# Expert weights applied on the way out of PSUM, results added to x by accumulating gathers, block scales on GpSimd, and weight rounding placed between the experts' tiles

## The chip, the cores and the metric

One core of a Trainium2 chip runs the whole kernel. The metric is the device time of one launch in microseconds (us); lower is better. The engines are TensorE (PE; its weight loads are PEld), VectorE (DVE), ScalarE (ACT), GpSimd (POOL) and SyncE (SP, which issues DMAs).

## What is computed

Four decoder layers on x of 8 sequences x 256 tokens x 256 features, all in 32 bit. Each layer adds self-attention, cross-attention and a feed-forward block to x. The change touches two neighbours: the feed-forward block of layer 1 (32 experts, the best 4 for each token, and a shared expert) and the attention of layer 2, whose operands are rounded to eight-bit floats in blocks of 128.

```python
def _L1_ffn_ref(x, ...):
    scores = softmax(flat @ router_w.T + router_bias)
    topk_scores, topk_idx = top_k(scores, 4)
    topk_scores = topk_scores / clip(topk_scores.sum(-1), 1e-12)
    h = silu(einsum('nd,ehd->neh', flat, gate_w)) * einsum('nd,ehd->neh', flat, up_w)
    expert_out = einsum('neh,edh->ned', h, down_w)
    sel = take_along_axis(expert_out, topk_idx[:, :, None], axis=1)
    out = (sel * topk_scores[:, :, None]).sum(axis=1)
    return out + silu(flat @ sgate_w.T) * (flat @ sup_w.T) @ sdown_w.T

def quant_dequant(x, maxval, fp8_dtype):          # blocks of 128, row-major
    s = max(abs(flat), axis=1) / maxval
    return (flat / s).astype(fp8_dtype).astype(float32) * s

def _L2_attn_ref(x, Wq, Wk, Wv, Wo, ln_w, ln_b):
    xn = fp8_layernorm(x, ln_w, ln_b)             # rounds its input (e4m3)
    q, k, v = (fp8_linear(xn, W) for W in (Wq, Wk, Wv))   # rounds xn and W (e4m3)
    qd, kd = qd_e5m2(rope(q)), qd_e5m2(rope(k))
    probs = softmax(qd @ kd.T / sqrt(D))
    return fp8_linear(probs @ v, Wo)
...
x = x + _L1_ffn_ref(layernorm(x), ...)
x = x + _L2_attn_ref(layernorm(x), ...)
```

## The kernel before

x stays in SBUF as eight tiles, one for each sequence, each of two halves of 128 tokens. The normalised x (xn) and its transpose (xnT) are also resident. Weights come through a ring of three slots.

The feed-forward block of layer 1 first writes xn to a table xd in HBM (one row for each token) and loads all experts' weights into one tile `wall`. `route` picks four experts for each token, gives each (token, expert) pair a place in a list sorted by expert, padded to tiles of 128 places, and makes three things: `place` (for each token, its four places), `token` (for each place, its token; 0 in places that nobody uses) and `who` (for each of the 96 tiles, the offset of its expert's weights). It also collects the four routing weights of each token in `w4`. Beside it the shared expert's sixteen steps run on TensorE, fourteen of them interleaved with the route by hand and two after the tiles.

`tiles_of_experts` then goes over the 96 tiles in a pipeline of four parts, each one step later than the one ahead of it: `turn` gathers 128 rows of xd (an indirect DMA that GpSimd issues) into xg and transposes them on TensorE, `widen` multiplies with gate and up weights whose offset TensorE reads from a register, `flip` transposes h, `narrow` multiplies with the down weights, copies the product out of PSUM on ACT as y, and SP writes y to a second table yd. In this stage only TensorE's order is fixed to program order; the other engines' instructions are ordered by the scheduler.

The attention of layer 2 is a list of generators, one for each sequence and one for rounding the weights. `staggered` runs them in turns: turn n takes one step of each work that has started, the oldest first; sequence b starts at turn 10 b, the weights at turn 0. Each `yield` ends a step. Here all four engines keep exactly the program's order (`in_order`; the profile shows these instructions under L71). A sequence's steps are: `expert_results` (eight gathers from yd into six buffers g, and eight VectorE steps that multiply with w4 and add to x), two rounds of moments, inverse root of the variance (GpSimd) and `e4m3` rounding, projections, rotation of q and k with the `scales` of e5m2 rounding, scores, softmax, values, `e4m3` again, output projection, and the statistics for the next layer. `scales` takes a block's largest magnitude, divides it by the format's largest number and inverts it, all on VectorE; `e4m3` is `scales`, four ACT steps (y = x times the inverse scale), four VectorE steps (rounding) and four ACT steps (times the scale), with a `yield` after each.

## Time and profile before

| | |
|---|---|
| three timed runs | 2462.15, 2464.55, 2473.96 us; median 2464.55 us |
| the profiled execution | 2461.47 us, span from first to last instruction 2459.7 us |
| busy in the span | PE 2217.8 (90%), DVE 1245.0 (51%), ACT 872.7 (35%), POOL 501.0 (20%) us |
| tiles of experts | first gather 1267.8 us, last write of y issued 1436.0 us |
| rounded attention | first gather from yd 1438.6 us, last statistics on GpSimd 1716.9 us |
| HBM traffic | 84.64 MB read, 16.78 MB written |

How to read the rows. A group has the line of the kernel, the engine and operation, the tiles written and read, shape and count; after the bar the busy time in us and the mean ns of one; after the second bar how long the engine had been idle just before, and what ended that. A wait row says which instruction waited for which: us in total, times, longest. A timeline row begins with the start and the length in us, and has the idle time before it in brackets. Busy shares are means over stages that have different owners, so each stage is looked at by itself.

### The profile page before, as it was taken

Reading aid. Unit: us, or ns where it says so; the run is one execution under the profiler, and the core shown is the slowest. Engines: PE = TensorE matmul, PEld = TensorE weight load, DVE = VectorE, ACT = ScalarE, POOL = GpSimd, SP = SyncE. Lnnn points to the kernel's source line nnn. Section 1 sums busy time; section 2 is a strip of 40 time slices with the busy share of each in tenths; the row PEclk is TensorE's granted clock in tenths of the full one; section 3 lists DMA queues with packets and bytes.
Section 4 is the critical chain, followed back from the end, with each engine's and each line's share of the span. In section 5 each row is a group of like instructions: output and inputs, shape, how many; then the busy total and the mean of one; then the engine's idle time right before and its main releaser. Section 6 shows DMA issues by size and latency. Waiting matters only on the chain. (4 is left out here: it accounts for less than half of the span.)

```text
span 2459.7 us, 31787 instructions
## 1 busy us (share of the span) xinstructions
PE 2217.8 (90%) x11611; PEld 1410.8 (57%) x11611; DVE 1245.0 (51%) x3192; ACT 872.7 (35%) x2118; POOL 501.0 (20%) x712
## 2 busy tenths in 40 slices
PE   7888889999999999899899955666999989999999
PEld 4555555666655555555568833444665555566556
DVE  5666553334323235676565558985453235555500
ACT  3433422334211113466113335664552114434311
POOL 3211333221000002221135534440222110000010
PEclk9999999999999999899899976886899998899999
DMA  3000000001100000121515643100111010000000
GB/s 128 1 1 1 30 14 26 18 10 41 52 13 26 13 18 13 48 66 36 210 53 165 153 95 104 46 18 14 49 39 32 1 52 10 18 18 18 3 13 22
DMA packets 56539, 103.68 MB, mean 42 GB/s; under 512 B 7624, under 2 KB 40224, under 8 KB 54720
## 3 DMA queue, kind: packets, MB, share of 16 engines
q1 hardware_dynamic: 44688, 75.90, 9.0%
q0 software_dynamic: 7680, 20.98, 3.7%
q10 hardware_dynamic: 4016, 4.76, 0.6%
q8 instruction: 94, 1.54, 0.3%
q14 instruction: 61, 0.50, 0.1%
HBM read 84.64 MB, written 16.78 MB: 41 GB/s over the span
## 5 line engine op out<-in xcount | busy, mean ns | idle before, releaser
L169 PE MATMUL mm<-xnT,w 128*128 128x512 f32 (+1 forms) x1104 | 475.3, 577 | 1.4 <-ACT xnT L252 0.7
L345 PE MATMUL mm<-kT,qT 17*128 17x256 f32 (+2 forms) x1536 | 322.4, 413 | 15.7 <-DVE q L363 12.7
L169 PEld LDWEIGHTS mm<-xnT,w 128*128 128x128 f32 x1104 | 210.6, 193 | 201.2 <-issue 192.1
L376 PE MATMUL mm<-qT,kT 18*128 18x256 f32 (+2 forms) x1536 | 309.5, 406 | 1.4 <-ACT p L388 1.2
L388 ACT ACTIVATE p<-mm 128x512 f32<-128x512 f32 (+1 forms) x384 | 212.1, 562 | 262.0 <-PE mm L376 137.1
L363 DVE TENSOR_REDUCE q<-mm 128x2 f32<-128x512 f32 x256 | 172.3, 688 | 164.1 <-PE mm L376 148.7
L345 PEld LDWEIGHTS mm<-kT,qT 17*128 17x128 f32 (+1 forms) x1536 | 179.1, 193 | 115.0 <-issue 41.3
L560 ACT ACTIVATE hT<-mm 128x512 f32<-128x512 f32 x104 | 62.1, 597 | 431.0 <-PE mm L169 416.6
L561 DVE TENSOR_TENSOR hT<-hT,mm 128x512 f32<-128x512 f32 x104 | 71.4, 687 | 278.2 <-PE mm L169 278.1
L536 PE MATMUL acc<-w,hT 128*128 128x256 f32 x832 | 195.5, 379 | 1.0 <-DVE x L271 1.0
L536 PEld LDWEIGHTS acc<-w,hT 128*128 128x128 f32 x832 | 157.9, 190 | 62.9 <-issue 41.6
L376 PEld LDWEIGHTS mm<-qT,kT 18*128 18x128 f32 (+1 forms) x1536 | 172.3, 191 | 13.2 <-issue 4.6
L235 POOL TENSOR_SCALAR rstd<-mv 128x2 f32<-128x2 f32 x64 | 12.3, 193 | 812.7 <-DVE mv L231 466.8
L399 PE MATMUL acc<-p,v 128*32 128x256 f32 (+2 forms) x1536 | 140.3, 386 | 0.0
L271 DVE TENSOR_TENSOR x<-x,mm 128x512 f32<-128x512 f32 x40 | 27.4, 686 | 193.1 <-PE mm L169 192.9
L297 ACT COPY qT<-tp 128x256 f32<-128x256 f32 x256 | 83.7, 375 | 84.0 <-PE tp L293 83.1
L1290 POOL DMA_INDIRECT xg<-xd,token x96 | 90.9, 947 | 87.8 <-PE tp L1413 54.2
L359 DVE TENSOR_REDUCE q<-mm 128x1 f32<-128x128 f32 (+1 forms) x256 | 78.7, 352 | 56.4 <-PE mm L334 56.1
L169 PE MATMUL mm<-wall,xT 128*128 x384 | 99.7, 383 | 1.1 <-DVE xT L1415 1.1
L293 PE MATMUL tp<-ident,q 128*128 128x128 f32 x512 | 90.6, 299 | 3.3 <-ACT qT L297 1.9
L399 PEld LDWEIGHTS acc<-p,v 128*32 128x32 f32 (+1 forms) x1536 | 61.1, 122 | 47.0 <-issue 21.5
L293 PEld LDWEIGHTS tp<-ident,q 128*128 128x128 f32 x512 | 60.7, 149 | 44.6 <-issue 32.0
(426 smaller groups left out, 3778.8 us busy)
## 6 DMA issues: line engine op xcount, KB each, us to landing
wall<-in_l1f_w SPq DMA_DIRECT2D x8, 1536.0 KB
yd<-y SPq DMA_DIRECT2D x96, 128.0 KB
kT<-in_ctxK SPq DMA_DIRECT2D x16, 512.0 KB
v<-in_ctxV SPq DMA_DIRECT2D x16, 512.0 KB
w<-in_l0f_w SPq DMA_DIRECT2D x8, 768.0 KB
cT<-in_ctxT SPq DMA_DIRECT2D x8, 512.0 KB
ctx<-in_ctx SPq DMA_DIRECT2D x8, 512.0 KB
w<-in_l2f_w SPq DMA_DIRECT2D x3, 768.0 KB
```

What stands on the lines that cost most here:

```text
L169: self.pe(self.nc.tensor.matmul(out, lhsT=lhsT, rhs=rhs, start=i == 0, stop=i == len(pairs) - 1))
L293: self.pe(self.nc.tensor.transpose(ps[:, i, t * P : (t + 1) * P], flat[:, t, g * P : (g + 1) * P], self.ident))
L297: self.nc.scalar.copy(dst, ps[:, i, :])
L345: self.pe(nc.tensor.matmul(ps[n][:, S * t : S * t + w], lhsT=qTs[n // hp][r, t * P : (t + 1) * P], rhs=kT[r, g, :w], start=t == 0 or not c ...
L359: self.dve(nc.vector.tensor_reduce(to[:, t : t + 1], bank[:, cols], axis=AX.X, op=ALU.max, negate=True))
L363: self.dve(nc.vector.tensor_reduce(to, bank.rearrange("p (t s) -> p t s", t=2), axis=AX.X, op=ALU.max, negate=True))
L376: self.pe(nc.tensor.matmul(ps[m, 1][:, 256 * k : 256 * k + w], lhsT=kT[r, g, k * P : (k + 1) * P], rhs=qTs[m // hp][r, S - w :], start=k = ...
L388: nc.scalar.activation(p, bank[:, :n3], AF.Exp, scale=scale)
L399: self.pe(nc.tensor.matmul(acc[r, S - w :], lhsT=v[:, k, (G * hp + i) % nh, :], rhs=live_p[G * hp + i][:, 256 * k : 256 * k + w], start=k ...
L536: self.pe(nc.tensor.matmul(acc[:, t, :], lhsT=hT[:, t * P : (t + 1) * P], rhs=units[i][2], start=i == 0 and t % 2 == 0, stop=i == len(unit ...
L561: nc.vector.tensor_tensor(hT, hT, u, ALU.mult)
L1290: (engine or self.nc.gpsimd).indirect_dma_start(out=dst, out_offset=None, in_=src, in_offset=bass.IndirectOffsetOnAxis(ap=rows, axis=0))
```

## The change

What it does, in five parts. The normalised routing weights (all 32 columns, zero where an expert was not chosen) are written to xd behind each token's features, so a row has 288 numbers; `who` gets a second row with the column of each tile's expert, which ACT loads into registers. `narrow` multiplies a row by its token's weight while it copies y out of PSUM; xg lives until then and has eight buffers instead of six, and y has two instead of three. `expert_results` becomes eight gathers from yd that add to x in the DMA; the buffers g and VectorE's part are gone. In `scales` the division and the inversion move to GpSimd (a multiplication and a power of -1), in its program order. The rounding of the attention's weights leaves the attention and runs in the tiles' loop, one step at every second tile from tile 16 on, in place in one ring slot, with the transposed result in a free part of xnT; two ring slots are no longer taken.

```diff
         self.minus = self.filled("minus", [P, 2], -0.5)
+        self.minus1 = self.filled("minus1", [P, 4], -1.0)
         self.eps5 = self.filled("eps5", [P, 1], 1e-5)
...
         return t
-    def slot(self):
-        return self.ring.tile([P, SLOT], F32, tag="w", name="w")
     def row(self, name, pool, dtype=F32):
...
         hbm, keep = self.hbm, self.between
-        xd = hbm.tile([N, D], F32, tag="xd", name="xd")
+        xd = hbm.tile([N, D + E], F32, tag="xd", name="xd")
         yd = hbm.tile([tiles * P, D], F32, tag="yd", name="yd")
...
         token = pool.tile([P, tiles], I32, tag="token", name="token", bufs=1)
-        who = pool.tile([1, P], I32, tag="who", name="who", bufs=1)
-        w4 = keep.tile([P, NT, K], F32, tag="w4", name="w4")
+        who = pool.tile([1, 2, P], I32, tag="who", name="who", bufs=1)
         for b in range(B):
             nc.sync.dma_start(
-                xd[b * S : (b + 1) * S].rearrange("(h p) d -> p h d", p=P), self.xn[:, 2 * b : 2 * b + 2, :]
+                xd[b * S : (b + 1) * S, :D].rearrange("(h p) d -> p h d", p=P), self.xn[:, 2 * b : 2 * b + 2, :]
             )
...
             self.pinned = True
-            steps = self.route(route, place, token, who, w4)
+            steps = self.route(route, place, token, who, xd)
             for n in range(14):
...
             pass
-        self.results = yd, place, w4
+        self.results = yd, place
     def expert_results(self, pool, b):
-        _, vector, _, gpsimd = self.in_order
-        yd, place, w4 = self.results
-        K = w4.shape[2]
-        got = []
-        for n in range(2 * K + 3):
-            if n < 2 * K:
-                g = pool.tile([P, D], F32, tag="g", name="g", bufs=6)
-                self.gather(g, yd, place[:, 2 * K * b + n : 2 * K * b + n + 1], gpsimd)
-                got.append(g)
-            if n >= 3:
-                t, k = 2 * b + (n - 3) // K, (n - 3) % K
-                xt = self.tile_of(t)
-                vector.scalar_tensor_tensor(xt, got[n - 3], w4[:, t, k : k + 1], xt, op0=ALU.mult, op1=ALU.add)
-            yield
-    def gather(self, dst, src, rows, engine=None):
+        yd, place = self.results
+        K = place.shape[1] // NT
+        for k in range(K):
+            for t in (2 * b, 2 * b + 1):
+                self.gather(self.tile_of(t), yd, place[:, K * t + k : K * t + k + 1], self.in_order[3], ALU.add)
+                yield
+    def gather(self, dst, src, rows, engine=None, op=ALU.bypass):
         (engine or self.nc.gpsimd).indirect_dma_start(
-            out=dst, out_offset=None, in_=src, in_offset=bass.IndirectOffsetOnAxis(ap=rows, axis=0)
+            out=dst, out_offset=None, in_=src, in_offset=bass.IndirectOffsetOnAxis(ap=rows, axis=0), compute_op=op
         )
-    def route(self, pool, place, token, who, w4):
+    def route(self, pool, place, token, who, xd):
...
                 self.pe(nc.tensor.matmul(tok, lhsT=hs, rhs=hi, start=n == 0, stop=n == NT * K - 1))
+            if g == 3:
+                self.normalise(pool, w, 1e-12)
+                nc.sync.dma_start(xd[:, D:].rearrange("(t p) e -> p t e", p=P), w)
             if g < 7:
...
         nc.vector.tensor_copy(token, tok)
-        e1 = new("e1", 1)
+        e1 = new("e1", 2)
         nc.vector.tensor_scalar(many, end, self.cst[:, C_PIDX : C_PIDX + 1], None, op0=ALU.is_le)
-        nc.vector.tensor_reduce(e1, many, axis=AX.X, op=ALU.add)
-        nc.vector.tensor_scalar(e1, e1, float(E - 1), 768.0, op0=ALU.min, op1=ALU.mult)
-        pe = self.turned(P)
-        self.pe(nc.tensor.transpose(pe[:1, :], e1, self.ident))
-        nc.vector.tensor_copy(who, pe[:1, :])
-        yield
-        self.normalise(pool, w, 1e-12)
-        for k in range(K):
-            same = pool.tile([P, NT, E], F32, tag="same", name="same", bufs=1)
-            nc.vector.tensor_tensor(same, at, best[:, :, k : k + 1].to_broadcast([P, NT, E]), ALU.is_equal)
-            nc.gpsimd.tensor_tensor(same, same, w, ALU.mult)
-            nc.vector.tensor_reduce(w4[:, :, k], same, axis=AX.X, op=ALU.add)
+        nc.vector.tensor_reduce(e1[:, :1], many, axis=AX.X, op=ALU.add)
+        nc.vector.tensor_scalar(e1[:, 1:], e1[:, :1], float(E - 1), float(D), op0=ALU.min, op1=ALU.add)
+        nc.vector.tensor_scalar(e1[:, :1], e1[:, :1], float(E - 1), 768.0, op0=ALU.min, op1=ALU.mult)
+        pe = self.turned(2, P)
+        for j in range(2):
+            self.pe(nc.tensor.transpose(pe[:1, j, :], e1[:, j : j + 1], self.ident))
+        nc.vector.tensor_copy(who, pe[:1])
+        yield
     def tiles_of_experts(self, pool, tiles, wall, token, who, xd, yd):
...
         G = 8
-        live = {}
-        value = {}
+        live, rows = {}, {}
+        value, column = {}, {}
         def turn(i):
-            xg = pool.tile([P, D], F32, tag="xg", name="xg", bufs=6)
+            xg = rows[i] = pool.tile([P, xd.shape[1]], F32, tag="xg", name="xg", bufs=8)
             self.gather(xg, xd, token[:, i : i + 1])
...
             if i % G == 0:
-                _, got = nc.values_load_multi_w_load_instructions(
-                    who[:, i : i + G], engines=[mybir.EngineType.PE], min_val=0, max_val=31 * 768,
-                    skip_runtime_bounds_check_because="a sum of 32 comparisons, and its minimum with 31",
-                )
-                value.update({i + j: v for j, v in enumerate(got)})
+                for j, into, engine, least, most in (
+                    (0, value, mybir.EngineType.PE, 0, 31 * 768), (1, column, mybir.EngineType.Activation, D, D + 31)
+                ):
+                    _, got = nc.values_load_multi_w_load_instructions(
+                        who[:, j, i : i + G], engines=[engine], min_val=least, max_val=most,
+                        skip_runtime_bounds_check_because="a sum of 32 comparisons, and its minimum with 31",
+                    )
+                    into.update({i + n: v for n, v in enumerate(got)})
             xT = live[i]
...
             self.mm(ps, (live.pop(i), wall[:, bass.ds(value[i] + 512, 256)]))
-            y = pool.tile([P, D], F32, tag="y", name="y")
-            nc.scalar.copy(y, ps)
+            y = pool.tile([P, D], F32, tag="y", name="y", bufs=2)
+            nc.scalar.activation(y, ps, AF.Identity, scale=rows.pop(i)[:, bass.ds(column[i], 1)])
             nc.sync.dma_start(yd[i * P : (i + 1) * P], y)
         self.pinned = True
+        weights = self.rounded_weights(pool)
         for n in range(tiles + 3):
+            if n >= 16 and n % 2 == 0:
+                next(weights, None)
             for late, part in enumerate((turn, widen, flip, narrow)):
...
-    def scales(self, vector, blocks, largest):
+    def scales(self, blocks, largest):
         nb = blocks.shape[1]
...
         r = self.small.tile([P, nb], F32, tag="qr", name="qr", bufs=8)
+        _, vector, _, gpsimd = self.in_order
         vector.tensor_reduce(s, blocks, axis=AX.X, op=ALU.max, apply_absolute_value=True)
-        vector.tensor_scalar_mul(s, s, 1.0 / largest)
-        vector.reciprocal(r, s)
+        gpsimd.tensor_scalar(s, s, 1.0 / largest, None, op0=ALU.mult)
+        gpsimd.tensor_tensor(r, s, self.minus1[:, :nb], ALU.pow)
         return s, r
-    def e4m3(self, pool, vector, scalar, dst, src):
+    def e4m3(self, pool, dst, src, bufs=(3, 2)):
         nb = src.shape[1]
-        s, r = self.scales(vector, src, 448.0)
-        yield
-        y = pool.tile([P, nb, P], F32, tag="qy", name="qy", bufs=3)
+        _, vector, scalar, _ = self.in_order
+        s, r = self.scales(src, 448.0)
+        yield
+        y = pool.tile([P, nb, P], F32, tag="qy", name="qy", bufs=bufs[0])
         for j in range(nb):
...
         yield
-        m = pool.tile([P, nb, P], F32, tag="qm", name="qm", bufs=2)
+        m = pool.tile([P, nb, P], F32, tag="qm", name="qm", bufs=bufs[1])
         vector.tensor_scalar(m.bitcast(I32), y.bitcast(I32), 0x7F800000, None, op0=ALU.bitwise_and)
...
         nc.gpsimd.memset(root, -0.5)
-        wT = self.slot()
         self.pinned = "all"
-        staggered(
-            (0, self.rounded_weights(pool, wT)),
-            *((10 * b, self.rounded_attention(pool, b, k_of(wT, 2), lnw, lnb, root)) for b in range(B)),
-        )
+        staggered(*((10 * b, self.rounded_attention(pool, b, self.wT, lnw, lnb, root)) for b in range(B)))
         self.pinned = False
-    def rounded_weights(self, pool, wT):
-        tensor, vector, scalar, _ = self.in_order
+    def rounded_weights(self, pool):
+        tensor, _, scalar, _ = self.in_order
         raw = self.weights(self.dram["l2a_w"])
-        rnd = self.slot()
+        self.wT = self.xnT[:, :, :1024]
         blocks = lambda a, i: a.rearrange("p (n i) -> p n i", i=P)[:, 4 * i : 4 * i + 4]
         for i in range(4):
-            yield from self.e4m3(pool, vector, scalar, blocks(rnd, i), blocks(raw, i))
-        r4 = rnd.rearrange("p (w o i) -> p w o i", w=4, o=2)
+            yield from self.e4m3(pool, blocks(raw, i), blocks(raw, i), (1, 1))
+        r4 = raw.rearrange("p (w o i) -> p w o i", w=4, o=2)
         for k in range(2):
...
                     tensor.transpose(tp[:, j * P : (j + 1) * P], r4[:, w + j // 2, j % 2, k * P : (k + 1) * P], self.ident)
+                scalar.copy(self.wT[:, k, w * D : (w + 2) * D], tp)
                 yield
-                scalar.copy(wT[:, k * 1024 + w * D : k * 1024 + (w + 2) * D], tp)
     def rounded_attention(self, pool, b, wk, lnw, lnb, root):
...
             )
-        yield from self.e4m3(pool, vector, scalar, xblk, xblk)
+        yield from self.e4m3(pool, xblk, xblk)
         mv = moments(xb)
...
             vector.scalar_tensor_tensor(xt, xt, rstd[:, t : t + 1], lnb, op0=ALU.mult, op1=ALU.add)
-        yield from self.e4m3(pool, vector, scalar, xblk, xblk)
+        yield from self.e4m3(pool, xblk, xblk)
         tp = turned(of(xb))
...
             vector.tensor_tensor(a[t][:, :, 1, :], a[t][:, :, 1, :], s[:, :, 0, :], ALU.add)
-            scale[t] = self.scales(vector, four(a[t]), 57344.0)
+            scale[t] = self.scales(four(a[t]), 57344.0)
         def narrow(t):
...
         oblk = o.rearrange("p t (n i) -> p (t n) i", i=P)
-        yield from self.e4m3(pool, vector, scalar, oblk, oblk)
+        yield from self.e4m3(pool, oblk, oblk)
         tp = turned(of(o))
```

## The prediction

> **What bounds the kernel now.** I read the row of slices first (TensorE is near 90% busy except for a dip between about 1450 and 1720 us), then cut that part into stretches. Columns: length, then busy time and instruction count of PE, PEld, DVE, ACT, POOL, then granted clock, DMA share, GB/s.
>
> ```profile
> 1285.00:1420.00 135.00, 134.12 (x740) 112.70 (x739) 74.48 (x245) 52.01 (x161) 77.68 (x83) 1.00 0.61 157
> 1455.00:1480.00 25.00, 4.82 (x14) 2.66 (x14) 22.65 (x54) 11.58 (x34) 13.90 (x15) 0.50 0.34 101
> 1560.00:1600.00 40.00, 29.47 (x107) 19.71 (x107) 38.17 (x97) 25.36 (x80) 19.21 (x22) 0.84 0.16 47
> 1600.00:1640.00 40.00, 21.57 (x74) 13.83 (x74) 38.04 (x98) 25.41 (x79) 16.14 (x20) 0.75 0.10 27
> 1680.00:1720.00 40.00, 24.62 (x78) 17.34 (x77) 16.96 (x42) 16.44 (x50) 2.69 (x6) 0.69 0.07 20
> ```
>
> Two stages have two owners. The experts' tiles (to 1436) belong to TensorE: 134 of 135 us. The rounded attention (1438 to 1717) belongs to VectorE: 38 of 40 us until 1640, then a thinning tail. GpSimd is half idle in it. Next, the groups of 1440 to 1720 (shape and count, busy us, mean ns, idle before), and two of GpSimd's groups over the whole span:
>
> ```profile
> L71 POOL DMA_INDIRECT g<-yd,place x63 | 65.7, 1043 | 26.5 <-issue 16.2 <-DVE x L71 9.7 <-DMA g<-yd,place 0.3
> L71 DVE TENSOR_TENSOR qy<-qy,qm 128x512 f32<-128x512 f32 x56 | 39.3, 701 | 1.9
> L71 DVE SCALAR_TENSOR_TENSOR x<-g,w,x 128x256 f32<-128x256 f32 x64 | 29.6, 465 | 0.3
> L71 DVE RECIPROCAL qr<-qs 128x4 f32<-128x4 f32 x44 | 7.8, 178 | 1.5
> L71 DVE TENSOR_SCALAR qs<-qs 128x4 f32<-128x4 f32 x44 | 7.5, 171 | 1.5
> ...
> L71 POOL TENSOR_TENSOR rs<-rs,minus 128x4 f32<-128x4 f32 x8 | 9.1, 1141 | 0.7
> L71 POOL TENSOR_SCALAR rs<-ss 128x4 f32<-128x4 f32 x8 | 2.2, 270 | 30.7 <-ACT junk L71 30.7
> ```
>
> The last two are the price of a block scale on GpSimd: the same shape, a multiply and a power. GpSimd's timeline gives the rhythm: each sequence's first inverse root of the norm.
>
> ```profile
> 1533.80 0.30 POOL L71 TENSOR_SCALAR frs<-fmv 128x2 f32<-128x2 f32 x1 [5.03 <-DVE fmv L71]
> 1560.63 0.30 POOL L71 TENSOR_SCALAR frs<-fmv 128x2 f32<-128x2 f32 x1 [4.50 <-DVE fmv L71]
> 1587.46 0.30 POOL L71 TENSOR_SCALAR frs<-fmv 128x2 f32<-128x2 f32 x1 [4.50 <-DVE fmv L71]
> 1614.28 0.30 POOL L71 TENSOR_SCALAR frs<-fmv 128x2 f32<-128x2 f32 x1 [4.49 <-DVE fmv L71]
> ```
>
> One sequence takes 26.8 us. VectorE's groups divided by eight give 28.0 us for one (22.5 without the weighted additions and the small scale steps), so VectorE sets the rhythm. Last, what the tiles' stage says of writes to yd: a wait row, two ACT lines, and the first gather from yd.
>
> ```profile
> ACT y L1445 <- DMA yd<-y: 12.5, 8, 3.7
> ...
> 1410.05 0.37 ACT L1445 COPY y<-mm 128x256 f32<-128x256 f32 x1 [0.63 <-DMA yd<-y]
> 1420.82 0.37 ACT L1445 COPY y<-mm 128x256 f32<-128x256 f32 x1 [3.74 <-DMA yd<-y]
> ...
> 1438.62 0.95 POOL L71 DMA_INDIRECT g<-yd,place  x1 [2.86 <-ACT hT L560]
> ```
>
> The last write of y is issued at 1436.0 and the gather that needs it starts at 1438.6: a lone write is usable after at most 2.6 us. In the busy end of the stage, a write issued at 1405.2 releases its buffer at 1410.05 (4.8 us), one issued at 1412.6 at 1420.8 (8.2). There the gathers xg land in 8.3 us (median), against 3.1 before: unused tiles all fetch one token's row.
>
> **The change, part by part. Tiles' stage.** y goes from three buffers to two. Copy i now waits until write i-2 has landed. Copy with a scale 0.42 (the pair o<-mm,den takes 0.84), hand-over to SP 0.03, write 2.95 (between the lone 2.6 and what gathers gain under load, 2.7 to 3.1) make 3.4 us for two tiles, 1.70 each, against the step of 1.63 in the timeline: 80 tiles x 0.07 = 6 us. In the slow end two writes of 5 to 6 us make 2.7 to 3.2 a tile, where three buffers gave 2.3 (1410.05 to 1426.21, seven steps): 12 tiles x 0.6 = 7 us. What waits behind y on ACT is the next h, then TensorE.
>
> The rounded weights come here. VectorE gets four times 0.68 + 2.28 us in blocks, ACT eight times 1.28, TensorE sixteen transposes of 0.275 (4.4 us). VectorE and ACT have 45% and 60% free, but a block of 2.28 beside the tile's own 1.0 passes the step, and TensorE's slack to xT is about 0.9: 4 x 0.8 = 3 us; half of the 4.4 hides under y's wait. I take 5 us. ACT's loads of column numbers (twelve of 0.59, the row of who on TensorE) and GpSimd's four scales hide while gathers run four tiles ahead (6.5 us, against a landing of 3.1); if not, they cost up to 7. xg rows of 1152 bytes for 1024: at most 12% of 3.1, in the same cover. Stage: +18, bounds +3 (y never waits, the rest covered) to +35.
>
> **Route.** Eight VectorE steps of 0.68 and four GpSimd steps of 1.27 go, a normalisation moves forward; TensorE is 84 of 87 us busy there, so 0. The write of weights (2048 pieces of 128 bytes on SP's queue) has about 20 us until the first gather; uncovered it would cost up to 10.
>
> **Attention.** VectorE loses 64 x 0.465 = 29.6, 44 x 0.35 = 15.3 (1.4 of it the weights'), and the weights' 4 x 2.95 = 11.8: 56.7 us. But all of GpSimd's work here is in program order. A scale is 0.27 + 1.14 + gaps = 1.7 us on it. A gather is 1.25 with its gap, eight per sequence, five scales, three roots of 1.25: 22 us of GpSimd per sequence, about VectorE's 22.5. And they are chained. Follow one round in the steady part, on GpSimd from the end of rotate(0): scale, gather, scale, gather, root, gather, root, scale, gather, scale, gather, that is 4 x 1.7 + 5 x 1.25 + 2.45 = 15.5 us without a pause. Then the last gather must land (2.9 and a hand-over, less 1.25: 1.85) before moments may start on VectorE (1.1); behind them queue another sequence's rounding (2.15), then xn 0.8, reduction 0.65, scale on GpSimd 1.55, ACT 1.3, rounding 2.15, the next rotate(0) 2.6: 14.2. With 0.4 of hand-overs the round is 30 us, not 26.8; VectorE sinks to about 70%.
>
> Before, gathers had six buffers of their own and ran ahead of VectorE; now each also waits for the gather two before it, into the same half of x. That hides at two steps (4 to 6 us) against 3.1.
>
> Rounds between first roots before: 20.8, 23.7, 24.1, three of 26.8, 31.2 (180.3). Walked the same way with fewer sequences under way: 22.4, 26.6, 28.8, four of 30 (197.8): +17.5. The start gains: eight gathers in two chains of four at 3.3 end at 1453, first root 1455.7 instead of 1465.2: -9.5. The tail has four scales at +1.3: +5. Accumulating reads the target too: no row shows it. At least 0 (a plain gather, 2.9; a gain is excluded, since it does more), at most +5.4 (a gather under full DMA load, 8.3); I take 0.5, near the plain row, eight times: +4. Its issue may cost 0.95 to 1.9; I take 0.95. Attention: +17, bounds -45 to +60. Earlier loads of the next layer's weights may meet the first gathers; bounded by one landing of 6.8, 4 us, in the range.
>
> **Two rules of the Trainium skill.** The rows say 0.35 us on VectorE against 1.41 on GpSimd, four times. The page GPSIMD Engine Reference, section Engine selection, says elementwise work of two inputs is about twice as slow there. By it the five scales of a round would be 3.5 us shorter, the round 26.5, the attention -4 and the whole +14; the row has the very shape, so I take the row. The page DMA: Bandwidth & Descriptors, section Rules for kernel authors, says that an accumulating DMA must wait for the semaphore of the earlier one to the same bytes. The trace has only plain gathers, issued 1.25 apart; by them alone eight would take 10 us at the start, by the rule 13 and more. I use the rule.
>
> **Sum.** 2461.5 (the profiled execution; span 2459.7) + 18 + 17 = 2496.5; the median of the runs (2464.55) lies 3 above this execution, of which I add half, since the lowest run (2462.15) lies at it: 2498.
>
> **The rivals.** (1) VectorE stays the only bound and relief is kept: 56.7 x 0.8 = -45, tiles +8: 2427. For it: 95% VectorE in the stretches. Against: the in-order GpSimd. It decides if the round falls below 26.8, that is if scales and gathers take under 12.3 us of GpSimd's 15.5. Chance 0.17. (2) Accumulation is slow: +4 per landing, seven rounds 28, start 16: 2542. For: nothing measured; against: 2.9 for a plain one. Chance 0.16. (3) The tiles' stage hides everything (write 2.6: two tiles in 3.05, under 3.26), attention costs little: +10: 2475. Chance 0.15. That x is tracked as a whole, so that all eight gathers wait in one chain, would add 2 us a round and belongs to (2). Mine: 0.52, own range 2478 to 2525.
>
> **Numbers.** A measurement of this kernel tells about 0.5% (12 us) from no change. Faster comes from (1), 0.17 and a little of (3): 0.18. Same (2452 to 2477): most of the lower half of (3), 0.10. Slower: 0.72. The range leaves out most of (1) and the top of (2): 2445 to 2550.
>
> **What would show it.** Right: first roots 30 us apart; VectorE near 28 of 40 us, GpSimd over 28; waits of moments on the gathers; y waiting for yd in most tiles, a tile step of 1.70. Wrong: roots 22 to 25 apart with VectorE still at 95% (rival 1), gathers landing in 6 us or more (rival 2), tile step 1.63 (rival 3).

## The result, and the profile after

The changed kernel takes 2543.18 us (median; 2531.71 to 2547.66). The kernel before took 2465.27 us on the same chip, so the ratio is 1.0302 (95%: 1.0271 to 1.0332). The profiled execution of the changed kernel took 2543.06 us, its span is 2541.3 us. I had forecast 2498 as the likeliest time, 2478 to 2525 if my own account held and 2445 to 2550 over all: the direction was right, the size was 33 us where 78 came.

Stretches of the changed kernel (length; busy time and count of PE, PEld, DVE, ACT, POOL; granted clock; DMA share; GB/s):

```profile
1285.00:1420.00 135.00, 127.01 (x687) 103.25 (x685) 77.69 (x245) 63.43 (x183) 76.82 (x82) 1.00 0.57 157
1560.00:1600.00 40.00, 23.21 (x72) 15.36 (x72) 24.01 (x55) 20.02 (x62) 26.31 (x28) 0.68 0.22 30
1600.00:1640.00 40.00, 24.27 (x78) 15.56 (x79) 25.10 (x57) 21.50 (x67) 27.42 (x28) 0.74 0.21 29
```

In the tiles' stage TensorE is no longer full: 127 of 135 us, for 134 before. In the attention VectorE fell from 38 to 25 of 40 us, and GpSimd rose from 19 to 27. No engine is full there, and it is slower all the same. Groups between 1440 and 1780 us (busy us, mean ns, idle before):

```profile
L71 POOL DMA_INDIRECT x<-yd,place x64 | 105.6, 1650 | 31.3 <-DMA x<-yd,place 17.7 <-issue 13.6
L71 POOL TENSOR_TENSOR qr<-qs,minus 128x4 f32<-128x4 f32 x40 | 43.9, 1097 | 3.3
...
L71 POOL TENSOR_SCALAR qs<-qs 128x4 f32<-128x4 f32 x40 | 13.6, 339 | 52.7 <-DVE qs L71 38.7 <-ACT o L71 7.2 <-ACT ra L71 3.1
```

The scales cost what the rows of before said (1.10 and 0.34 us for 1.14 and 0.27). The issue of an accumulating gather does not: 1.65 us of GpSimd, where a plain one took 1.04. GpSimd's timeline shows the rhythm, by the first root of each sequence:

```profile
1564.88 0.30 POOL L71 TENSOR_SCALAR frs<-fmv 128x2 f32<-128x2 f32 x1 [3.02 <-DVE fmv L71]
...
1598.16 0.30 POOL L71 TENSOR_SCALAR frs<-fmv 128x2 f32<-128x2 f32 x1 [2.95 <-DVE fmv L71]
...
1631.81 0.30 POOL L71 TENSOR_SCALAR frs<-fmv 128x2 f32<-128x2 f32 x1 [3.03 <-DVE fmv L71]
...
1665.12 0.30 POOL L71 TENSOR_SCALAR frs<-fmv 128x2 f32<-128x2 f32 x1 [2.98 <-DVE fmv L71]
```

A round is 33.4 us on average, for 26.8 before. GpSimd's part of the one that ends at 1631.81, from the end of the first half's rotation to the next first root:

```profile
1610.08 0.23 POOL L71 TENSOR_SCALAR qs<-qs 128x4 f32<-128x4 f32 x1 [0.70 <-DVE qs L71]
1610.39 1.05 POOL L71 TENSOR_TENSOR qr<-qs,minus 128x4 f32<-128x4 f32 x1
1611.63 1.65 POOL L71 DMA_INDIRECT x<-yd,place  x1 [0.19 <-issue]
1614.05 0.23 POOL L71 TENSOR_SCALAR qs<-qs 128x4 f32<-128x4 f32 x1 [0.77 <-ACT ra L71]
1614.36 1.05 POOL L71 TENSOR_TENSOR qr<-qs,minus 128x4 f32<-128x4 f32 x1
1615.60 1.80 POOL L71 DMA_INDIRECT x<-yd,place  x1 [0.19 <-issue]
...
1618.71 1.86 POOL L71 DMA_INDIRECT x<-yd,place  x1 [0.19 <-issue]
...
1623.24 1.68 POOL L71 DMA_INDIRECT x<-yd,place  x1 [0.17 <-issue]
1624.36 1.01 POOL L71 TENSOR_SCALAR qs<-qs 128x4 f32<-128x4 f32 x1
1625.45 1.48 POOL L71 TENSOR_TENSOR qr<-qs,minus 128x4 f32<-128x4 f32 x1
1627.12 1.66 POOL L71 DMA_INDIRECT x<-yd,place  x1 [0.19 <-issue]
1631.81 0.30 POOL L71 TENSOR_SCALAR frs<-fmv 128x2 f32<-128x2 f32 x1 [3.03 <-DVE fmv L71]
```

It is the order of scales, gathers and roots that the prediction walked, each gather longer than it was priced: from 1610.08 to the end of the last issue (1628.78) 18.7 us pass, for the 15.5 of the walk; the rest of the round takes 15.0, for 14.6. From the last gather's start to the root, 4.7 us pass: the landing, then the statistics on VectorE.

Something else is in the trace that the prediction has no term for. Stretches of the cross-attention that follows, in the changed kernel:

```profile
1780.00:1800.00 20.00, 19.37 (x74) 12.69 (x76) 5.43 (x8) 4.48 (x11) 0.00 (x0) 0.51 0.01 2
...
1820.00:1840.00 20.00, 20.00 (x88) 12.79 (x88) 6.43 (x15) 6.49 (x15) 3.69 (x3) 0.50 0.10 27
```

and in the kernel before:

```profile
1718.00:1738.00 20.00, 19.78 (x82) 13.02 (x82) 7.09 (x10) 5.08 (x12) 0.00 (x0) 0.54 0.01 2
1738.00:1758.00 20.00, 20.00 (x162) 13.86 (x162) 10.49 (x25) 11.54 (x28) 6.14 (x5) 1.00 0.17 54
```

TensorE is busy throughout, but at a granted clock of 0.50 it does 88 matmuls in 20 us, not 160. Before, that ended after some 18 us; here it lasts some 60.

At the start of the rounded attention the gathers wait for one another's landings. Those into the first half of x, in a second profile of the changed kernel:

```profile
1449.42 1.61 POOL L71 DMA_INDIRECT x<-yd,place  x1 [3.93 <-issue]
...
1456.29 1.53 POOL L71 DMA_INDIRECT x<-yd,place  x1 [3.37 <-DMA x<-yd,place]
...
1463.85 1.53 POOL L71 DMA_INDIRECT x<-yd,place  x1 [4.19 <-DMA x<-yd,place]
...
1470.99 1.53 POOL L71 DMA_INDIRECT x<-yd,place  x1 [3.38 <-DMA x<-yd,place]
```

The next layers' loads run beside them. In the first profile they make 223 GB/s (last column), where the prediction's stretch from 1455 had 101:

```profile
1451.00:1478.00 27.00, 7.70 (x28) 4.94 (x26) 5.23 (x8) 0.60 (x1) 12.33 (x8) 0.72 0.81 223
```

Profile against profile (us):

| part | before | after | difference |
|---|---|---|---|
| start to first gather xg | 1267.8 | 1261.2 | -6.6 |
| first xg to first gather from yd | 170.8 | 189.7 | +18.9 |
| first gather from yd to first root | 26.6 | 27.9 | +1.3 |
| first root of sequence 0 to that of 7 | 180.3 | 221.2 | +40.9 |
| from there to the first scores of the cross-attention | 72.7 | 80.6 | +7.9 |
| first scores to first addition to x | 32.6 | 44.9 | +12.3 |
| rest | 708.9 | 715.7 | +6.8 |
| span | 2459.7 | 2541.3 | +81.6 |

The two differences ahead of the last row, 19 us, are the slow clock: in a second profile of the changed kernel (below), where the slow clock was short, these parts took 32.5 and 708.7 us.

### The profile page after: what moved, and what is told of

The parts are those of the page before. It is cut to its first block, busy times and chain, and to the rows that moved or that the text cites. A ratio compares the mean times of both kernels' runs of the same rounds, so it can differ in the third digit from the quotient of the medians.

```text
span 2541.3 us, 31871 instructions
## 1 busy us (share of the span) xinstructions
PE 2244.5 (88%) x11612; PEld 1419.9 (56%) x11612; DVE 1198.9 (47%) x3034; ACT 878.3 (35%) x2118; POOL 594.2 (23%) x796
## 4 chain that ended last, share of the span: by engine, by line
PE 70%; DVE 11%; POOL 6%; issue 5%; DMA 4%; ACT 3%; ACTq 0%; POOLq 0%; SPq 0%; DVEq 0%
PE mm L167 29%; PE mm L343 8%; PE mm L71 6%; PE acc L534 6%; PE acc L397 5%; PE mm L374 4%; PE tp L291 3%; PE tp L71 3%; DMA x<-yd,place 2%; POOL x L71 2%; PE mm L332 2%; POOL qr L71 1%; DVE xn L71 1%; PE mm L416 1%; PE acc L71 1%
## 5 line engine op out<-in xcount | busy, mean ns | idle before, releaser
L343 PE MATMUL mm<-kT,qT 17*128 17x256 f32 (+2 forms) x1536 | 333.5, 421 | 15.9 <-DVE q L361 12.7
L374 PE MATMUL mm<-qT,kT 18*128 18x256 f32 (+2 forms) x1536 | 320.8, 415 | 1.5 <-ACT p L386 1.2
L343 PEld LDWEIGHTS mm<-kT,qT 17*128 17x128 f32 (+1 forms) x1536 | 185.4, 198 | 118.3 <-issue 44.5
L233 POOL TENSOR_SCALAR rstd<-mv 128x2 f32<-128x2 f32 x64 | 12.3, 193 | 815.5 <-DVE mv L229 466.1
L374 PEld LDWEIGHTS mm<-qT,kT 18*128 18x128 f32 (+1 forms) x1536 | 179.0, 195 | 15.1 <-issue 4.9
L397 PE MATMUL acc<-p,v 128*32 128x256 f32 (+2 forms) x1536 | 145.8, 394 | 0.0
L71 POOL DMA_INDIRECT x<-yd,place x64 | 105.6, 1650 | 31.3 <-DMA x<-yd,place 17.7
L397 PEld LDWEIGHTS acc<-p,v 128*32 128x32 f32 (+1 forms) x1536 | 62.8, 124 | 49.4 <-issue 23.8
```

The source lines that it names most:

```text
L71: ins = getattr(self.engine, name)(*args, **kwargs)
L343: self.pe(nc.tensor.matmul(ps[n][:, S * t : S * t + w], lhsT=qTs[n // hp][r, t * P : (t + 1) * P], rhs=kT[r, g, :w], start=t == 0 or not c ...
L374: self.pe(nc.tensor.matmul(ps[m, 1][:, 256 * k : 256 * k + w], lhsT=kT[r, g, k * P : (k + 1) * P], rhs=qTs[m // hp][r, S - w :], start=k = ...
L397: self.pe(nc.tensor.matmul(acc[r, S - w :], lhsT=v[:, k, (G * hp + i) % nh, :], rhs=live_p[G * hp + i][:, 256 * k : 256 * k + w], start=k ...
```

## The experiments

Each kernel is the changed kernel with the edit shown, cut to its main lines, unless said otherwise. Times are medians, ratios are to the kernel before on the same chip; intervals are 95%. "Rounds" are the distances of first roots in the steady part, "stretch" is the time from the first scores of the cross-attention to the first addition to x. In profiles of kernels without idle matmuls the stretch varies from 32.3 to 44.9 us, so edits are compared by rounds and not by the whole time alone.

**Scales back on VectorE.**

```diff
-        gpsimd.tensor_scalar(s, s, 1.0 / largest, None, op0=ALU.mult)
-        gpsimd.tensor_tensor(r, s, self.minus1[:, :nb], ALU.pow)
+        vector.tensor_scalar_mul(s, s, 1.0 / largest)
+        vector.reciprocal(r, s)
```

> The changed kernel with one part undone: the two small steps of a block scale (multiply, reciprocal) are VectorE's again; gathers accumulate as in the change. Theory A (GpSimd's program order sets the round of 33.3 us between first roots, scales and gathers both in it): a round loses four scales of 1.7 us from GpSimd's chain and gets about 1.5 us of hand-overs and VectorE work back, so about 28 us, the attention about 38 us shorter, the kernel near 2505. Rival B (the accumulating gathers alone set the round, by issue and landing): rounds stay at 32 to 33 and the time near 2540. Rival C (scales alone set it): rounds near 25, the time near 2485.

**Plain gathers, VectorE adds.**

```diff
+                g = pool.tile([P, D], F32, tag="g", name="g", bufs=6)
-                self.gather(self.tile_of(t), yd, ..., self.in_order[3], ALU.add)
+                self.gather(g, yd, ..., gpsimd)
...
+                vector.tensor_tensor(xt, xt, got[n - 3], ALU.add)
```

> The changed kernel with another part undone: results are gathered plainly into six buffers, running ahead, and VectorE adds each to x (already weighted, so an addition of two inputs instead of the multiply-add); scales stay on GpSimd. Theory A: issue 1.65 becomes 1.0 for five gathers in the chain (-3), the last landing and its wait leave the chain (-2 to -4), VectorE gets eight additions of about 0.35 us (+1): a round of about 28, the kernel near 2505. Rival B (accumulating gathers alone): rounds near 25, near 2480. Rival C (scales alone): rounds 32 to 33, near 2540.

**Both of these edits.**

> Both parts undone at once: scales on VectorE, plain gathers with an addition by VectorE. Left of the change are the weighting as results leave PSUM, two y buffers, and the weights rounded between the tiles. All theories: VectorE is the bound again, about 28.0 less 1.5 (the weights' rounding) less 8 x 0.1 (addition for multiply-add), rounds near 25.5, attention some 60 us shorter than the change's: near 2485 if the slow clock after the attention stays (20 us), near 2465 if it goes.

The first took 2479.37 us (1.0067; 1.0049 to 1.0086), the second 2489.82 (1.0122; 1.0084 to 1.0160), both together 2452.97 (0.9966; 0.9954 to 0.9978). One stretch, 1560 to 1600, of the three in this order:

```profile
1560.00:1600.00 40.00, 23.16 (x80) 15.84 (x79) 33.10 (x84) 25.91 (x80) 24.06 (x21) 0.76 0.24 34
```

```profile
1560.00:1600.00 40.00, 20.25 (x68) 12.72 (x68) 31.61 (x76) 24.17 (x76) 26.65 (x36) 0.71 0.12 34
```

```profile
1560.00:1600.00 40.00, 27.62 (x103) 18.40 (x101) 38.11 (x102) 27.07 (x85) 15.93 (x20) 0.87 0.15 45
```

Rounds are 28.3, 28.8 and 26.3 us. With both undone, VectorE fills 38 of 40 us again. With one part alone neither engine is full (33 and 24; 32 and 27). From 26.3, accumulation alone adds 2.0 and the scales alone 2.5, but both together 7.1. My reading is that the first part hides in what VectorE still needed and the second finds that cover used up; the sums show that the costs don't add, not why. Neither part alone sets the round, so rivals B and C of these texts fall. The times of the first two came 15 to 26 us under the 2505 expected, in part because the stretch was 39.6 and 32.5 us for 44.9. With plain gathers the start, from the first gather from yd to the first root, is 18.7 us for 27.9.

**The gathers write over x.**

```diff
-                self.gather(self.tile_of(t), yd, ..., self.in_order[3], ALU.add)
+                self.gather(self.tile_of(t), yd, ..., self.in_order[3])
```

> The changed kernel with its gathers writing over x instead of adding to it (the experts' sums are left out); order, waits and bytes written stay. My sum priced the gather so: 0.95 for its issue, 2.9 for its landing. If the accumulation itself is the mis-sized term (five issues at 0.7 more on the chain): issues near 1.0, rounds near 30, about 25 us under the changed kernel. If a gather's issue is long because it waits or depends on the one before: issues stay at 1.6 and rounds at 33.

2501.96 us (1.0171; 1.0127 to 1.0215), with a stretch of 32.5. Its group of gathers between 1440 and 1780:

```profile
L71 POOL DMA_INDIRECT x<-yd,place x64 | 71.9, 1124 | 31.9 <-DMA x<-yd,place 17.1 <-issue 14.8
```

Order and waits are those of the change, and the issue is 1.12 us for 1.65. Two first roots of its timeline:

```profile
1574.10 0.30 POOL L71 TENSOR_SCALAR frs<-fmv 128x2 f32<-128x2 f32 x1 [2.58 <-DVE fmv L71]
...
1605.12 0.30 POOL L71 TENSOR_SCALAR frs<-fmv 128x2 f32<-128x2 f32 x1 [2.58 <-DVE fmv L71]
```

31.0 us; on average 30.8, for 33.4. GpSimd's walk is 16.5 us in this round (1586.04 to 1602.54), for 18.7, and the rest 14.5, for 15.0. So it is the accumulation that makes the issue long, not the wait before it; with an issue near the price that it was given, the chain comes near the 30 that was forecast. From issue to landing a gather takes 3.0 us here (median), 3.9 where it accumulates, 2.9 plain.

**Gathers spread out.**

```diff
                 yield
+                if b:
+                    yield
...
-(10 * b, self.rounded_attention(...))
+(10 * b - 8 * (b > 0), self.rounded_attention(...))
```

> The changed kernel with its accumulating gathers, from the second sequence on, begun eight steps earlier and two steps apart instead of one, so that a gather no longer waits for the landing of the one before it into the same half of x, nor the norm for the last one. Every instruction stays. Theory A (landings are links of GpSimd's chain): the waits of 3.3 (norm on the last landing) and about 1.5 on the gathers go, a round of 33.3 becomes 28.5 to 30, the time 20 to 28 us under the changed kernel's. Rival B (the instructions' own time on GpSimd: 1.65 for an issue, 1.4 for a scale): rounds stay at 32 to 33, the time within 8 us.

2522.84 us (1.0205; 1.0175 to 1.0236). Rounds are 32.2 to 32.7, as rival B expected. The waits for landings do go. Between 1560 and 1640 the changed kernel's statistics wait so:

```profile
DVE fst L71 <- DMA x<-yd,place: 10.9, 6, 3.3
```

Here no row of waits names a gather, and the round gives back only 1 us. Profile against profile, both with a stretch of 44.9, this kernel is 12 us shorter, where rival B allowed 8: the first root of sequence 7 comes 9.6 us sooner after that of sequence 0, 3.8 of it in the last round.

**Two of five scales back on VectorE** (those of queries and keys).

```diff
-            scale[t] = self.scales(four(a[t]), 57344.0)
+            scale[t] = self.scales(four(a[t]), 57344.0, True)
```

> The changed kernel with two of the five block scales of a sequence (those of queries and keys) on VectorE again. If each instruction on GpSimd's queue stands in the round for its whole length (theory of the chain): 2 x 1.7 less 2 x 0.35, so 30 to 30.6 for 33.3, and about 22 us less in all. If the relief only comes with the last of them (a threshold): rounds stay at 32 to 33.

2529.12 us (1.0225; 1.0163 to 1.0287). Rounds are 31.7, a fall of 1.7 where 2.8 to 3.4 was expected and where a threshold would have given none. Removing all five gave 5.1. So a scale stands in the round for 0.9 to 1.1 us, not for its whole 1.7: the round is not one chain without slack.

**Half of the additions by the gathers**, all scales on VectorE.

```diff
+            if n < K:
+                self.gather(self.tile_of(t), yd, ..., gpsimd, ALU.add)
+            elif n < 2 * K:
+                g = pool.tile([P, D], F32, tag="g", name="g", bufs=6)
+                self.gather(g, yd, ..., gpsimd)
...
+                vector.tensor_tensor(xt, xt, got[n - K - 3], ALU.add)
```

> Half of the gathers' additions left to the accumulating gathers (the first two experts of each row), the other half gathered plainly and added by VectorE; all block scales on VectorE. Against the version with plain gathers and VectorE's scales (rounds 26.3, VectorE 95% busy) VectorE loses four additions of 0.42 us a round, and GpSimd gets four issues of 1.6 for 1.0. If VectorE is the bound there: rounds near 24.6 to 25.5 and about 8 us under that version's ratio of 0.997. If GpSimd's order sets in already: rounds of 26.3 or more and no gain.

2460.36 us (0.9980; 0.9967 to 0.9992). Rounds are 26.2, as with plain gathers, though VectorE lost four additions of 0.41 us. VectorE is still 37 of 40 us busy, and four issues on GpSimd take 1.63 us for 1.00. The trade is no gain; what VectorE's relief would be worth alone, this run does not show.

**Next layers' loads held back.**

```diff
+        self.held = [self.ring.tile([P, SLOT], F32, tag="w", name="w") for _ in range(2)]
+        for t in self.held:
+            self.in_order[3].memset(t[:, :1], 0.0)
...
+        for t in self.held if b == 0 else ():
+            gpsimd.tensor_copy(small("held", 1), t[:, :1])
```

> The changed kernel with the next layers' loads (weights of 0.75 MB and 3 MB of keys and values) held back until the first sequence's first root, by two ring slots that are kept until then; in the kernel before they came at about the same point, as the rounding of weights held these slots. If these loads are what stretched the eight first gathers (6.5 to 7.8 us a landing), the start of 27.9 us becomes 18 to 20 and the time falls by 8 to 10. If the first landings are slow by themselves, start and time stay within 2 us.

2537.71 us (1.0277; 1.0252 to 1.0302): no gain. The start falls from 27.9 to 21.6 us, a little less than expected, but the next round is 32.3 instead of 25.4. Its gathers, held back on GpSimd by landings:

```profile
1456.22 1.53 POOL L71 DMA_INDIRECT x<-yd,place  x1 [1.17 <-DMA x<-yd,place]
...
1460.27 1.53 POOL L71 DMA_INDIRECT x<-yd,place  x1 [0.68 <-DMA x<-yd,place]
...
1470.81 1.67 POOL L71 DMA_INDIRECT x<-yd,place  x1 [0.18 <-issue]
...
1479.17 1.55 POOL L71 DMA_INDIRECT x<-yd,place  x1 [4.48 <-DMA x<-yd,place]
```

Without the loads, one half of x takes a new gather every 4.05 us (1456.22 to 1460.27); once they run, 8.4 pass (1470.81 to 1479.17). So accumulating gathers take longer beside the loads; moved to a later point, the loads meet those of the next sequence.

**Tiles' stage: three buffers for y** (and seven for xg, for space).

```diff
-            xg = rows[i] = pool.tile([P, xd.shape[1]], F32, tag="xg", name="xg", bufs=8)
+            xg = rows[i] = pool.tile([P, xd.shape[1]], F32, tag="xg", name="xg", bufs=7)
...
-            y = pool.tile([P, D], F32, tag="y", name="y", bufs=2)
+            y = pool.tile([P, D], F32, tag="y", name="y", bufs=3)
```

> The changed kernel with three buffers for y in place of two, and seven for xg in place of eight to make room. By my sum y's second buffer cost 13 of the tiles' stage's 18 us: the stage 187 to about 174, the time near 2530. If the rounding of weights between the tiles is what costs, the stage stays at 185 to 187 and the time within 2 us.

2528.82 us (1.0285; 1.0257 to 1.0312), not to be told from the changed kernel. The stage is 185.9 us, inside the 181.4 to 189.7 that the changed kernel's own tiles took in eight profiles (the change twice, and six of the experiments that leave the tiles alone). The changed kernel had this row of waits:

```profile
ACT y L1436 <- DMA yd<-y: 29.9, 23, 3.7
```

In the experiment it is gone, and gathers wait longer for y's copies (28.6 us in the changed kernel), as xg lives until then and has one buffer fewer:

```profile
POOL xg L1280 <- ACT y L1436: 69.2, 80, 4.1
```

So y's wait is real, but without it the stage is no shorter here. The number of xg buffers was changed with it and may have taken a gain, so this does not clear y's second buffer.

**A fixed column for the weight.**

```diff
-                for j, into, engine, least, most in (
-                    (0, value, mybir.EngineType.PE, 0, 31 * 768), (1, column, mybir.EngineType.Activation, D, D + 31)
-                ):
+                for j, into, engine, least, most in ((0, value, mybir.EngineType.PE, 0, 31 * 768),):
...
-            nc.scalar.activation(y, ps, AF.Identity, scale=rows.pop(i)[:, bass.ds(column[i], 1)])
+            nc.scalar.activation(y, ps, AF.Identity, scale=rows.pop(i)[:, D : D + 1])
```

> The changed kernel with the column of the weight fixed (the first of the 32) instead of loaded into ScalarE's registers, so the weighting uses one expert's weight for all tiles; everything else stays. My sum hid these loads, with up to 7 us if they do not hide. If they set the tile step of 1.75 (1.63 before): steps of 1.65 to 1.68 and the tiles' stage 7 to 9 us shorter. If y's two buffers, or the longer copy, do: the stage within 3 us.

2530.01 us (1.0231; 1.0197 to 1.0265); the stage is 184.4 us, again inside that spread, so for the stage it is inconclusive. But its median step from one copy of y to the next is 1.63 us, as in the kernel before, for 1.70 and 1.71 in the two profiles of the changed kernel, and 1.70 with three buffers for y.

**The kernel before with only the rounding of weights moved between the tiles.**

```diff
+        weights = self.rounded_weights(pool)
         for n in range(tiles + 3):
+            if n >= 16 and n % 2 == 0:
+                next(weights, None)
...
-            (0, self.rounded_weights(pool, wT)),
```

> The kernel before with one part of the change alone: the weights of the rounded attention are rounded between the experts' tiles. Weighting, gathers and scales as before. By my sum the tiles' stage grows by about 5 us; the start of the attention falls from 26.6 to about 18 (no blocks of weights ahead of the first sequence), rounds stay at 26.8: about 4 to 8 us under the kernel before. If the rounding is what made the tiles' stage 19 us longer: no gain, up to 10 us slower.

2461.95 us (0.9986; 0.9972 to 1.0001): as before, or a little faster. The tiles' stage is 177.9 us (+7.1), the start of the attention 19.4 (-7.2), rounds 26.8. What it takes in one place it gives in the other.

**The slow clock: TensorE kept busy.**

```diff
+        def warm():
+            for n in range(24):
+                self.in_order[0].matmul(self.bank(512), lhsT=self.ident, rhs=self.cst[:, :512], start=True, stop=True)
+                yield
...
+        staggered(..., (96, warm()))
```

> The changed kernel with 24 idle matmuls of 128x512 (nobody reads them) put one to a step into the last sequence's steps, so that TensorE is nearly busy up to the end of the attention. In its profile TensorE then stays at half clock for 60 us of the cross-attention, which costs about 20 us against the profile of before. If the thinly used TensorE of the attention's end is the cause: the clock is near 1.00 from the first scores on, the stretch from the first score to the first addition to x falls from 44.9 to 32 or less, the end of the attention grows by 2 to 8 us, and the time falls by 8 to 15. If the slow clock has another cause: 44.9 stays and the time grows by 2 to 8.

**The changed kernel once more.**

> The changed kernel as it is, once more, for its second profile: rounds of 33.3 again if the order of instructions sets them. The cross-attention's stretch is either 44.9 us again (then the slow clock comes with this kernel) or 32 to 33 (then it comes and goes, and this execution is 12 to 20 us shorter).

With the idle matmuls: 2513.91 us (1.0194; 1.0162 to 1.0226); without: 2537.70 (1.0297; 1.0263 to 1.0332). The start of the cross-attention with them, and then a stretch of the second profile without:

```profile
1776.00:1800.00 24.00, 23.58 (x182) 16.39 (x184) 12.22 (x22) 12.81 (x31) 2.46 (x2) 1.00 0.08 23
```

```profile
1800.00:1820.00 20.00, 20.00 (x164) 13.68 (x162) 10.35 (x25) 11.07 (x27) 5.88 (x7) 1.00 0.16 54
```

With the matmuls the stretch is 23.8 us, and the attention's end is 2 us longer. The unedited kernel's stretch was 32.5 this time, its rounds again 33.4 to 33.6: the half clock is sometimes short and sometimes long in executions of the same kernel. The mean clock fits that (two of them: 2522.07 us at 0.928, 2544.00 at 0.915).

**The same 24 matmuls in the kernel before, and in the version with both parts undone** (from turn 99 on, for 96).

> The kernel before with the same 24 idle matmuls. Its stretch of 32.6 us holds some 9 us of half clock: 24 with them, and 5 to 9 us less in all, if the clock is lost in the thinning end of the attention whatever the change; else 0 to 4 us more.

> The version that was faster than both (plain gathers, VectorE's scales, weighting at PSUM, weights rounded between the tiles), with the 24 idle matmuls one to a step in the last sequence's steps. Its cross-attention stretch of 36.3 us should fall to about 24, its time by 8 to 14: near 0.992 of the kernel before. If only the changed kernel's longer end profits: no gain over 0.997.

Before, with them: 2453.89 us (0.9959; 0.9940 to 0.9977), the stretch 23.8 for 32.6. The version with both parts undone: 2447.25 us (0.9932; 0.9913 to 0.9952), the stretch 23.8 for 36.3. That is the fastest kernel of this study; it keeps from the change the weighting at PSUM, y's two buffers and the rounding between the tiles.

## Why the prediction was right or wrong

Its direction and the order that it walked on GpSimd held; the step that failed is the price of an accumulating gather, and a term for the clock was missing.

- **The round (forecast 30, measured 33.4): the mis-sized term is the gather's issue**, "I take 0.95", from bounds of 0.95 to 1.9. It is 1.65. Five of them in the walked order are 5 x 0.70 = 3.5, and 30 + 3.5 = 33.5. The overwriting gathers show that term: 1.12 us, rounds of 30.8. Over the seven rounds that makes +40.9 for +17.5, half of the miss. That the sum agrees so closely is in part luck. At 1614.05 GpSimd waits 0.77 us for the second half's rotation, so the gather at 1611.63 hides, and what makes up for it is the last one's longer landing and a scale that was stretched. Spreading the gathers out and returning two scales also moved the round less than a chain without slack would.
- **The landing (0.5 over a plain one)** measured 3.9 for 2.9 (medians from issue), so 1.0. In the steady part it counts little: without its waits the round fell by 1 us. The rule that a gather must await the earlier one was used rightly and shows in the group's 17.7 us of waits for x<-yd.
- **The start (forecast -9.5, measured +1.3): "two chains of four at 3.3" failed.** Gathers came 6.5 to 7.8 us apart in each chain, and the next layers' loads came 16 us earlier (1451.8 for 1467.4), as, by the code, the rounding of weights no longer held ring slots. With the loads held back, the first gap of a chain was still 6.6, the later ones 4.0 to 4.5. The prediction named the loads and bounded them by "one landing of 6.8, 4 us"; they meet several in a row. The chain counts too: plain gathers, which need not wait for one another, gave a start of 18.7.
- **The end of the attention** grew by 7.9 for 5.
- **The clock: a missing term, 19 us in the profiled execution.** The prediction asked what each engine does and not in which clock the attention leaves TensorE to the next layer. With idle matmuls in the attention's end the stretch is 23.8 us in three kernels, so a fuller TensorE there keeps the clock; the kernel before loses about 9 us there too. What makes the half clock last 18 or 60 us stays open.
- **The tiles' stage** came out at 18.9 for 18, and that is luck: the same tiles took 181.4 to 189.7 us in eight profiles, that is +10.6 to +18.9, and the parts don't bear it out. The rounding costs 7 (forecast 5). The 13 us for y's second buffer did not show when the third came back. The forecast step of 1.70 us came, but with three buffers for y too, and not with a fixed column; y waited for yd in 23 of 96 tiles, not in most. How the rest divides between weighting, registers, y and GpSimd's scales stays open.
- **The rivals.** Rival 2 came near in time (2542), and near in where it put it: 28 us more on the seven rounds and 16 on the start, where 23.4 and 10.8 came. But a landing is 1.0 us longer and not 4; in the rounds it is the issue on GpSimd that costs, and gaps over 6 us in a chain came only at the start and beside the loads. Rival 1 needed scales and gathers in under 12.3 us of GpSimd; they took 18.7, and VectorE fell to 25 of 40 us. Rival 3 fell with the stage's +10.6 at least and the rounds.
- **The rules.** The Trainium skill's page GPSIMD Engine Reference, section Engine selection, about twice as slow for elementwise work of two inputs, would have given 26.5; the row of the very shape (1.41 against 0.35) held, at 1.44 after. What the prediction makes of the rule for the whole (-4 and +14) is loose: 3.5 us over seven rounds are 24.5, so -7.5 and +10.5.

Profile against profile the miss is 81.6 - 35 = 46.6 us: 23.4 in the rounds, 10.8 at the start, 19.1 by the clock, 2.9 at the end and 0.9 in the tiles, less 6.6 that came ahead of the tiles and the 4 that the forecast had set aside for landings. In the second profile, where the slow stretch was as short as before, the parts are these: 10.8 up to the first gather from yd, 1.4 start, 40.9 rounds, 7.7 end, together 60.8; its span is 60.6 us over that of before.

## What to carry to other kernels

Before work moves off a full engine, write down the order in which the receiving queue will run it and price every instruction there with a row of its own kind; if there is none, as for an accumulating gather here, the far end of the bound deserves as much weight as the near one. Two parts that each cost little alone need not add: here 2.0 and 2.5 became 7.1, I think because they used up the same cover. Look at the granted clock behind a stage that thins out: 24 idle matmuls at its end were worth about 8 to 24 us in three kernels (by their ratios to the kernel before).

## What the runs showed of the hardware

- An indirect gather that adds to SBUF keeps GpSimd 1.65 us, one that overwrites the same bytes with the same waits 1.12 us; from issue to landing they take 3.9 and 3.0 us (medians). A new accumulating gather into the same bytes starts 4.05 us after the one ahead of it without the next layers' loads, and 6.7 to 8.4 us after it beside them.
- TensorE stayed at half clock through some 60 us in which it was busy without a pause with matmuls of which over half had 33 or 34 rows of 128 (L343 and L374). With 24 full matmuls of 128 rows among the work before, it ran at 1.00 through the same work, 54% of it with such few rows as well. The Trainium skill's page TensorE: Matmul & The Clock Gate, Part 1, says that about 3.4 us of sustained work release the clock; here 18 and 60 us of it passed first in two kernels, and no run tells what ended the half clock.
- A multiplication of 128x4 on GpSimd took 0.23 us alone and 1.01 at 1624.36, the power after it 1.48 for 1.05. The first begins inside a gather's issue (1623.24 to 1624.92); whether that stretched it was not tried.
